# Gate logits of the last layer for seven of eight token groups, moved beside the second image's scan

## The chip, the cores and the metric

The kernel runs on one core of one Trainium2 chip, as one launch. The metric is device time in microseconds (us), and a kernel's time is the median of its runs. Everything is in float32.

## The reference, cut to what matters

The model takes two images of 128 channels on 64 x 64 points (4096 tokens each) through two layers. Layer 0 has a deformable convolution and a small mixture of experts. Layer 1 has a selective scan over the 4096 tokens and then the expert block that this change touches:

```
# layer 1: the scan, then the experts
x = x + _L1_conv_ref(_ln_c(x), ...)            # scan over tokens; its sum is x3 in the kernel
t = _to_tokens(x)
t = t + _L1_ffn_ref(_ln_t(t), gate_w, gate_b, weight1, weight2)

# _L1_ffn_ref, with 64 experts and K = 8
logits = einsum('bsd,ed->bse', x, gate_w) + gate_b
probs = softmax(logits, axis=1)                # over all 4096 tokens
vals, idx = top_k(probs.transpose(0, 2, 1), K) # eight tokens for each expert
pooled = einsum('bked,bke->bed', gathered, topv)
h = gelu(einsum('ebd,edh->ebh', [pooled, 1], weight1))
out = einsum('ebh,eho->ebo', [h, 1], weight2)
outputs[topi] += out * topv
```

The softmax runs over tokens, so it needs the logits of all tokens, and their maximum. The norm, the transposes and the logits of a token need that token alone.

## The kernel before

**The stages.** The deformable convolution of both images comes first. Then `L1Conv.scan` (L1549) runs over 16 pieces `k` of 512 tokens: pieces 0 to 7 are image 0, pieces 8 to 15 image 1. While image 0 is scanned, the rest of image 1's layer 0 and its first steps of layer 1 run beside it (the list `rest`). While image 1 is scanned, only work for its own next piece runs beside it. Last comes `L1Ffn.run`: the gate, the experts and the output.

**The scan loop.** Each piece has 32 units (two halves of 128 channels, 16 states each). A unit `u` issues, in this order: the scan itself on DVE (L1668); `drive(u + 3)`, a product on POOL (L1580); the copy of a state on POOL (L1677); `decay(u + 2)`, an exponential on ACT (L1587) into one of two PSUM tiles `da`; four transposes on PE of the unit before (`turn`, L120, two PSUM tiles `ht`); and `weigh(u - 2)`, a product with C, which for image 1 is one quarter on DVE (L1614) and three quarters on ACT (L1616). PE then adds the weighted tiles up by further transposes into `py` (L1625). Each engine takes its instructions in the order in which they were issued.

**The side work of the scan.** After these, a unit takes steps from a list `side` of generators: two steps a unit, and four in piece 7 once `rest` is done. Each generator stands for one piece of work and gives way at every `yield`:

- `prepare(k + 1)` (L1467) makes the next piece ready. It has 11 empty steps (L1485), then loads `zz` and `sab` and takes 37 more steps: eight convolution matmuls on PE (L1444), sigmoids on ACT (L1451 to L1459), products on POOL (L1462), the projection `px` on PE (L1500) and its copy on ACT (L1503), further small matmuls, then a softplus made of squares on ACT (L1537) and products on DVE (L1530 to L1544), and two products on POOL (L1547).
- `project(k - 1)` (L1701) is put ahead of it at unit 5 of each piece. It has five steps: a load of `xr`, 16 matmuls on PE (L1710), two empty steps, and an add on DVE (L1720) with the store of the 512 tokens to the tensor `x3` in device memory (L1721).

At unit 28 the list is drained, whatever is left in it. `prepare` has 48 steps and `project` five, so at two steps a unit they end in unit 26.

The transfers are issued on SP's queue, in order: among them are the rows `bcb` (L1598), one for each unit and eight units deep, each of which waits for a free buffer, so that SP is some five units ahead of the scan.

**Weights ahead.** The 64 experts' weights come in 16 chunks of four experts, 1 MB each, for `weight1` and again for `weight2`. A pool of `EARLY` = 9 buffers is opened during image 1's scan, and `ahead` (called every 24 units, L1664) loads a chunk into it. A pool of `LATE` = 4 buffers is loaded in the gate stage. So 13 chunks are in place or on their way when the experts begin, and the other 19 are loaded as buffers come free.

**The gate** (L1820). It loads all of `x3` in 16 transfers, then for each of eight groups of 512 tokens and each image takes the norm of the tokens (`token_norm`, L94 to L107, with a square root on ACT, L81), four transposes (L120), a copy (L1857) and a matmul with the gate weights (L1858); then the bias on ACT (L1861) and the group's maximum on DVE (L1847). Next come the maximum over the groups (L1867), one exponential over all logits (L1870), the eight largest (L1871, L1873), and the pooling of tokens (L1878 to L1897). This last part of the program, `L1Ffn.run`, is not in the order that is written by hand: there the framework orders the instructions.

Three helpers matter:

```
def rstd_gen(nc, out, var, eps):
    nc.vector.tensor_scalar(out, var, eps, None, ALU.add)
    nc.scalar.activation(out, out, AF.Sqrt)
    yield
    yield
    nc.vector.reciprocal(out, out)
```

`token_norm_gen` issues four pairs of `bn_stats` and `bn_aggr`, then the lines above, then four `tensor_scalar` and one `yield`; `token_norm` runs it through at once.

Of the kernel before, what the change touches and what calls it, by code (L numbers as in the profile page):

```python
# [19 lines left out]
P = 128  # L20
B = 2
# [4 lines left out]
GT = 4  # L26
# [86 lines left out]
def token_norm(*args):  # L113
    for _ in token_norm_gen(*args):
        pass
# [999 lines left out]
class L1Conv:  # L1115
# [351 lines left out]
    def prepare(self, b, k, sp, pp, res):  # L1467

        env, nc = self.env, self.env.nc
        l0 = k * LC  # L1470
        bank = lambda shape, name: pp.tile(shape, F32, name=name, tag="m")
        wk = lambda name: sp.tile([P, 2, LC], F32, name=name, tag="wk", bufs=3)
        xc = sp.tile([P, 2, LC + 3], F32, name="xc", bufs=1)
        xsd = self.xsd[b].rearrange("(h p) l -> p h l", p=P)
        if k:
            nc.sync.dma_start(out=xc, in_=xsd[:, :, l0 - 3 : l0 + LC])
        else:
            nc.gpsimd.memset(xc[:, :, 0:3], 0.0)
            nc.sync.dma_start(out=xc[:, :, 3:], in_=xsd[:, :, 0:LC])

        def gap(n):
            for _ in range(n):
                yield

        yield from gap(11)  # L1485
        zz = sp.tile([P, 2, LC], F32, name="zc")
        nc.sync.dma_start(out=zz, in_=self.zsd[b].rearrange("(h p) l -> p h l", p=P)[:, :, l0 : l0 + LC])
        sa = sp.tile([P, LC], F32, name="sab", tag="one", bufs=1)
        nc.sync.dma_start(out=sa, in_=self.sad[b][0, l0 : l0 + LC].partition_broadcast(P))

# [36 lines left out]
        nc.scalar.activation(e, v, AF.Abs)  # L1527
        nc.scalar.activation(e, e, AF.Exp, scale=-1.0)
        yield from gap(3)
        nc.vector.tensor_scalar(q, e, LINEAR[0], LINEAR[1], ALU.mult, ALU.add)  # L1530
        yield
        nc.vector.tensor_tensor(q, q, e, ALU.mult)
        dl = sp.tile([P, 2, LC], F32, name="delta")
        du = sp.tile([P, 2, LC], F32, name="du")
        ts = [dl, du] * 2
        for i, (sc, _, add) in enumerate(SQUARES):
            nc.scalar.activation(ts[i], e, AF.Square, bias=self.sqb[:, i : i + 1], scale=sc)  # L1537
            yield
# [12 lines left out]
    def scan(self, sp, ps, pp, rest, ahead):  # L1551
# [87 lines left out]
        def project(k):  # L1639
            return self.project(k // NK, k % NK, pieces[k]["zz"], sp, pp)  # L1640
# [11 lines left out]
        for u, (k, half, n) in enumerate(units):  # L1652
            state = states[k // NK]
            if k and half == 0 and n == 5:
                side.todo.appendleft(project(k - 1))
            last = n == DS - 4 and half == 1
            if last and k == NK - 1:
                rest.drain()
# [3 lines left out]
                side.add(gen)  # L1662
            fetch(u + BCB - 2)
            if k >= NK and u % 24 == 12:  # L1664
                ahead()

            hs[u] = sp.tile([P, LC], F32, name="h", bufs=3)
            nc.vector.tensor_tensor_scan(  # L1668
# [17 lines left out]
            if n == DS - 1:  # L1686
                adds.append((u + 4, gate, u))

            for _ in range(2 if rest.todo or k != NK - 1 else 4):
                side.step()  # L1690
            credit += 1
            while credit > 0 and rest.todo:
# [51 lines left out]
EC = 4  # L1744
EQ = 16
NHC = HID // P
EARLY = 9
LATE = 4


class L1Ffn:
# [1 line left out]

    def __init__(self, env, ctx):
        self.env, self.ctx = env, ctx
        self.early, self.w1 = None, []

    def fetch(self, pool):  # L1760
# [7 lines left out]
    def ahead(self):  # L1768

        if self.early is None:  # L1770
            self.early = self.ctx.enter_context(self.env.tc.tile_pool(name="f1x", bufs=EARLY, side="right"))
        if len(self.w1) < EARLY:
            self.fetch(self.early)

    def run(self, x3, out):
        tc, nc, d = self.env.tc, self.env.nc, self.env.d
        env = self.env
        with ExitStack() as ctx:
# [23 lines left out]
            with (  # L1802
# [3 lines left out]
                for i, (b, g) in enumerate(work):  # L1806
# [10 lines left out]
                    nc.vector.tensor_copy(so, flat)  # L1817
                    nc.sync.dma_start(out=out[b, :, g * 512 : (g + 1) * 512], in_=so)

    def gate(self, x3, G, s1, pd, late):  # L1820


        env, tc, nc, d = self.env, self.env.tc, self.env.nc, self.env.d
        with (
            tc.tile_pool(name="f1r", bufs=1) as rp,
            tc.tile_pool(name="f1s", bufs=2) as sp,
            tc.tile_pool(name="f1p", bufs=2, space=PSUM) as pp,
        ):
            xn = rp.tile([P, NT, B, C], F32, name="xn")
            for g in range(NG):  # L1830
                for b in range(B):
                    cut = slice(g * GT, (g + 1) * GT)
                    nc.sync.dma_start(out=xn[:, cut, b, :], in_=x3[b][:, cut, :])
            for _ in range(LATE):
                self.fetch(late)
            gw = rp.tile([P, B, B, E1], F32, name="gw")
            nc.gpsimd.memset(gw, 0.0)
            for b in range(B):
                nc.scalar.dma_start(out=gw[:, b, b, :], in_=d["gate_w"])
            gb = rp.tile([P, 1], F32, name="gb")  # L1840
            for b in range(B):
                nc.scalar.dma_start(out=gb[b * E1 : (b + 1) * E1, :], in_=d["gate_b"])
            lg = rp.tile([P, N], F32, name="lg")
            mx = rp.tile([P, NG], F32, name="mx")

            def largest(g):
                nc.vector.tensor_reduce(mx[:, g : g + 1], lg[:, g * 512 : (g + 1) * 512], AX.X, ALU.max)  # L1847

            for g in range(NG):
                pl = pp.tile([P, 512], F32, name="pl")  # L1850
                for b in range(B):
                    dst = xn[:, g * GT : (g + 1) * GT, b, :]
                    token_norm(env, sp, "n3", dst, dst, 1e-5)
                    pb = pp.tile([P, GT, P], F32, name="pb")
                    transpose4(nc, env.ident, pb, [dst[:, j, :] for j in range(GT)])
                    xnt = sp.tile([P, 512], F32, name="xnt")
                    nc.scalar.copy(xnt, pb.rearrange("p j t -> p (j t)"))  # L1857
                    nc.tensor.matmul(  # L1858
                        pl, gw[:, b, :, :].rearrange("p k e -> p (k e)"), xnt, start=b == 0, stop=b == B - 1
                    )  # L1860
                nc.scalar.activation(lg[:, g * 512 : (g + 1) * 512], pl, AF.Identity, bias=gb)  # L1861
                if g:
                    largest(g - 1)
            largest(NG - 1)
            m8 = rp.tile([P, 8], F32, name="m8")

            nc.vector.tensor_reduce(s1, mx, AX.X, ALU.max)  # L1867
# [117 lines left out]
def metaformer_kernel(ctx: ExitStack, tc: tile.TileContext, d: dict, out: bass.AP):  # L1985
# [2 lines left out]
    tile_d = lambda shape, name: [dp.tile(shape, F32, name=f"{name}{b}", tag=f"{name}{b}") for b in range(B)]  # L1988
    x2, x3 = tile_d([P, NT, C], "x2_"), tile_d([P, NT, C], "x3_")
    keep = ctx.enter_context(tc.tile_pool(name="keep", bufs=1))  # L1990
    last = L1Ffn(env, ctx)
    with tc.manual_schedule(engines={ET.PE, ET.DVE, ET.Activation, ET.Pool, ET.SP}), ExitStack() as l0:
        mixer = L1Conv(env, dp, keep, x2, x3)
        mixer.room = lambda: ctx.enter_context(tc.tile_pool(name="wd", bufs=1, side="right"))
# [14 lines left out]

        conv = L0Conv(env, l0)  # L2010
        conv.run(chain(mixer.constants(), position_matrices(env, mixer.pos)), after)
        mixer.run(functools.partial(after, 1), last.ahead)
    last.run(x3, out)


# [83 lines left out]
```

## Time and profile before

| | us |
|---|---|
| median of three runs (7286.02 to 7301.13) | 7298.4 |
| the profiled execution's own time | 7266.68 |
| its span, from the first to the last instruction | 7264.9 |
| image 1's first piece (k = 8), from 6449.9 | 74.6 |
| pieces 9 to 14, each | 72.3 to 75.1 |
| piece 15, from 6965.5 | 46.8 |
| gate: norms, logits and maxima, 7025.8 to 7072.1 | 46.3 |
| gate: softmax, eight largest, pooling, 7072.1 to 7112.3 | 40.2 |
| experts, from the first matmul at 7117.0 to 7237.2 | 120.2 |
| output, to the end | 27.7 |

A piece is counted from its first scan to the next piece's first scan. Times in the profile count from the first instruction. In a line of the timeline the first number is the start, the second the duration, then come the engine, the line, the operation and what it writes and reads; in square brackets stand the idle time of the engine before it and what ended it. In a line of a stretch (from:to) stand, for each engine, its busy time with the number of instructions, then the granted TensorE clock, the share of DMA time and GB/s.

### The profile page before, as it was taken

How to read it: one execution, taken by the hardware profiler on the slowest of the kernel's cores; microseconds unless marked ns; L12 is line 12 of the kernel's file. 1: busy time of each engine (PE TensorE's matmuls, PEld its weight loads, DVE VectorE, ACT ScalarE, POOL GpSimd, SP SyncE). 2: the span in 40 equal slices, each digit the busy share in tenths (PEclk: the TensorE clock that was granted, in tenths of full speed). 3: DMA queues.
4: the chain of work that ended last, by engine and by line, in shares of the span. 5: the costliest groups of instructions: out<-in, count | busy, mean ns of one | idle time of the engine just before them, and what ended most of it. 6: DMA issues, size and time to landing. Idle time of an engine off the chain costs nothing.

```text
span 7264.9 us, 72120 instructions
## 1 busy us (share of the span) xinstructions
PE 5060.9 (70%) x22497; PEld 3188.1 (44%) x22497; DVE 5800.1 (80%) x6710; ACT 2259.9 (31%) x4642; POOL 5081.6 (70%) x5062
## 2 busy tenths in 40 slices
PE   4667677777777665766666776766547888867768
PEld 3444444444444442333333443443224567755544
DVE  5988888888888887898988888788866766677871
ACT  2211111111111112311111222121118877677860
POOL 4777777777777777777777777777765345567840
PEclk8888898898888988988889888888878888888889
DMA  7887777777777778877777888878765234544545
GB/s 221 276 286 227 231 224 231 218 238 224 232 229 222 232 218 275 293 239 230 232 229 220 254 249 242 243 244 250 230 187 180 79 106 130 147 144 156 169 137 162
DMA packets 667321, 1550.06 MB, mean 213 GB/s; under 512 B 181668, under 2 KB 230988, under 8 KB 666940
## 3 DMA queue, kind: packets, MB, share of 16 engines
q0 software_dynamic: 307200, 1006.88, 46.0%
q1 hardware_dynamic: 330812, 490.87, 21.2%
q10 hardware_dynamic: 28928, 47.70, 1.8%
q8 instruction: 182, 2.98, 0.2%
q14 instruction: 199, 1.63, 0.1%
HBM read 1436.70 MB, written 110.84 MB: 213 GB/s over the span
## 4 chain that ended last, share of the span: by engine, by line
PE 45%; issue 20%; DVE 10%; DMA 10%; POOL 7%; ACT 6%; SPq 2%; ACTq 0%; DVEq 0%; POOLq 0%
PE out L799 20%; PE pst L120 6%; POOL v L731 6%; DMA v<-table,idx 6%; PE po L428 5%; DVE v L772 2%; DVE h L1668 2%; ACT w L1616 2%; PE ps L1234 1%; PE ht L120 1%; DVE v L774 1%; PE ps L1247 1%; PE px L1028 1%; PE py L1625 1%; PE pfo L875 1%
## 5 line engine op out<-in xcount | busy, mean ns | idle before, releaser
L731 POOL DMA_INDIRECT v<-table,idx x3840 | 4085.1, 1064 | 1264.4 <-issue 990.0
L772 DVE TENSOR_TENSOR v<-v,pw 128x2048 f32<-128x2048 f32 x960 | 2192.3, 2284 | 620.8 <-DMA v<-table,idx 561.7
L799 PE MATMUL out<-st,regw 128*128 128x512 f32 x3840 | 2213.5, 708 | 89.7 <-ACT ys L813 84.6
L779 ACT COPY st<-pst 128x512 f32<-128x512 f32 x960 | 561.7, 585 | 3967.3 <-PE pst L120 3947.6
L120 PE MATMUL pst<-ident,v 128*128 128x128 f32 x3840 | 690.0, 309 | 1556.9 <-issue 1374.1
L120 PEld LDWEIGHTS pst<-ident,v 128*128 128x128 f32 x3840 | 473.3, 156 | 1989.1 <-issue 1755.7
L774 DVE TENSOR_TENSOR v<-v 128x1024 f32<-128x1024 f32 x960 | 1176.9, 1226 | 33.1
L799 PEld LDWEIGHTS out<-st,regw 128*128 128x128 f32 x3840 | 787.4, 228 | 696.8 <-issue 587.1
L1580 POOL TENSOR_TENSOR db<-du,bcb 128x512 f32<-128x512 f32 x512 | 670.1, 1309 | 510.1 <-DVE h L1668 382.7
L1668 DVE TENSOR_TENSOR_SCAN h<-da,state,db 128x512 f32<-128x512 f32 x512 | 652.0, 1273 | 85.2 <-ACT da L1587 53.8
L775 DVE TENSOR_TENSOR v<-v 128x512 f32<-128x512 f32 x960 | 664.2, 692 | 33.0
L120 PE MATMUL ht<-ident,h 128*128 128x128 f32 x2048 | 364.6, 307 | 235.6 <-ACT w L1616 211.3
L1587 ACT ACTIVATE da<-delta,w_A_log 128x512 f32<-128x512 f32 x512 | 359.9, 703 | 220.0 <-DVE h L1668 216.3
L120 PEld LDWEIGHTS ht<-ident,h 128*128 128x128 f32 x2048 | 262.7, 157 | 364.4 <-ACT w L1616 301.0
L1616 ACT ACTIVATE w<-ht,ct 128x128 f32<-128x128 f32 x1280 | 384.1, 371 | 21.9 <-DVE w L1614 21.5
L428 PEld LDWEIGHTS po<-wa,win 128*128 128x128 f32 x2112 | 323.2, 200 | 96.2 <-issue 96.2
L1614 DVE TENSOR_TENSOR w<-ht,ct 128x256 f32<-128x256 f32 (+1 forms) x512 | 173.7, 339 | 230.6 <-PE ht L120 228.3
L428 PE MATMUL po<-wa,win 128*128 128x147 f32 x2112 | 345.2, 296 | 0.0
L1625 PE MATMUL py<-ident,w 128*128 128x128 f32 x2048 | 338.3, 296 | 0.0
L1625 PEld LDWEIGHTS py<-ident,w 128*128 128x128 f32 x2048 | 274.1, 156 | 23.0 <-issue 22.7
L1234 PEld LDWEIGHTS ps<-ipw,hs 128*120 128x120 f32 x1408 | 180.7, 196 | 86.3 <-ACT X L1181 55.4
L1234 PE MATMUL ps<-ipw,hs 128*120 128x128 f32 x1408 | 188.8, 287 | 40.8 <-ACT X L1181 35.8
(327 smaller groups left out, 5189.2 us busy)
## 6 DMA issues: line engine op xcount, KB each, us to landing
bcb<-bc SPq DMA_DIRECT2D x512, 256.0 KB
regw<-in_regw SPq DMA_DIRECT2D x192, 640.0 KB
v<-table,idx POOLq DMA_INDIRECT x3840
yd<-ys ACTq DMA_DIRECT2D x128, 256.0 KB
yc<-yd SPq DMA_DIRECT2D x16, 2048.0 KB
wt<-in_weight SPq DMA_DIRECT2D x32, 1024.0 KB
tm<-pos SPq DMA_DIRECT2D x32, 720.0 KB
pos<-zero SPq DMA_DIRECT2D x48, 240.0 KB
```

Of the source, the lines that this page charges most:

```text
L120: nc.tensor.transpose(ps[:, j, :], s, ident)
L428: m()
L731: self.env.nc.gpsimd.indirect_dma_start(out=v[:, j, :], out_offset=None, in_=self.table[b], in_offset=bass.IndirectOffsetOnAxis(ap=idx[:, ...
L772: nc.vector.tensor_tensor(v4, v4, w, ALU.mult)
L774: nc.vector.tensor_tensor(up, up, v4[:, :, 2:4, :], ALU.add)
L775: nc.vector.tensor_tensor(v4[:, :, 0, :], v4[:, :, 0, :], v4[:, :, 1, :], ALU.add)
L779: nc.scalar.copy(st, pt.rearrange("p j t -> p (j t)"))
L799: nc.tensor.matmul(self.out[half], self.regw[t // CH][:, t % CH, half * P : (half + 1) * P], st, start=first, stop=last,)
L1580: nc.gpsimd.tensor_tensor(dbs[u], pieces[k]["du"][:, half, :], rows.pop(u), ALU.mult)
L1616: nc.scalar.activation(ws[u][:, j, :], ht[:, j, :], AF.Copy, scale=ct[:, j, n : n + 1])
L1625: nc.tensor.matmul(py[k][:, j * P : (j + 1) * P], w[:, j, :], env.ident, is_transpose=True, start=False, stop=n == DS - 1 and j == GT - 1,)
L1668: nc.vector.tensor_tensor_scan(hs[u], das.pop(u), dbs.pop(u), state[:, half, n : n + 1], ALU.mult, ALU.add)
```

## The change

The norms, transposes, logits and maxima of the first seven groups are taken out of the gate and made a generator `logits(g)`, which joins the side list of the scan. It is added at unit 5 of pieces 9 to 15, for the group of the piece before (`g = k - 9`), behind whatever is in the list. It has 16 steps: the loads of both images' `x3` slices and four steps' wait; for each image the statistics and the root, an empty step, the reciprocal and the scalings, the transposes, and the copy; then both matmuls in one step, the bias in one, the maximum in one. The gate itself keeps group 7.

In pieces 9 to 15 a unit takes three side steps for two. For the pieces prepared there, `prepare` has 18 empty steps at its start for 11.

The pools of the gate (normed tokens `xn`, gate weights, logits, maxima) are opened in image 1's first piece, and their gate weights are loaded there on SP's queue (before: ACT's, in the gate). To make room, `EARLY` is 5 for 9, and `LATE` is 6 for 4: 11 chunks ahead for 13.

```diff
-        yield from gap(11)
+        yield from gap(18 if b and k > 1 else 11)
...
                 side.todo.appendleft(project(k - 1))
+                if k > NK:
+                    side.add(ahead.logits(k - 1 - NK, pp, "m"))
...
-                ahead()
+                ahead.ahead()
...
-            for _ in range(2 if rest.todo or k != NK - 1 else 4):
+            for _ in range((3 if k > NK else 2) if rest.todo or k != NK - 1 else 4):
                 side.step()
...
-EARLY = 9
-LATE = 4
+EARLY = 5
+LATE = 6
...
+    def logits(self, g, pp, tag=None):
+        env, nc, sp = self.env, self.env.nc, self.gp
+        bank = lambda shape, name: pp.tile(shape, F32, name=name, tag=tag or name)
+        cut = slice(g * GT, (g + 1) * GT)
+        for b in range(B):
+            nc.sync.dma_start(out=self.xn[:, cut, b, :], in_=self.x3[b][:, cut, :])
+        for _ in range(4):
+            yield
+        xnt = []
+        for b in range(B):
+            dst = self.xn[:, cut, b, :]
+            yield from token_norm_gen(env, sp, "n3", dst, dst, 1e-5)
+            pb = bank([P, GT, P], "pb")
+            transpose4(nc, env.ident, pb, [dst[:, j, :] for j in range(GT)])
+            yield
+            xnt.append(sp.tile([P, 512], F32, name="xnt"))
+            nc.scalar.copy(xnt[b], pb.rearrange("p j t -> p (j t)"))
+        yield
+        pl = bank([P, 512], "pl")
+        for b in range(B):
+            nc.tensor.matmul(pl, self.gw[:, b, :, :].rearrange("p k e -> p (k e)"), xnt[b], start=b == 0, stop=b == B - 1)
+        yield
+        at = self.lg[:, g * 512 : (g + 1) * 512]
+        nc.scalar.activation(at, pl, AF.Identity, bias=self.gb)
+        yield
+        nc.vector.tensor_reduce(self.mx[:, g : g + 1], at, AX.X, ALU.max)
+        yield
...
     def gate(self, x3, G, s1, pd, late):
...
-            tc.tile_pool(name="f1r", bufs=1) as rp,
-            tc.tile_pool(name="f1s", bufs=2) as sp,
+            self.gates,
...
             for _ in range(LATE):
                 self.fetch(late)
...
-            for g in range(NG):
-                pl = pp.tile([P, 512], F32, name="pl")
...
-            largest(NG - 1)
+            for _ in self.logits(NG - 1, pp):
+                pass
```

More of the change, by code (lines that the diff above doesn't have):

```diff
@@ L1746, with __init__ @@
 NHC = HID // P
-EARLY = 9
-LATE = 4
+EARLY = 5
+LATE = 6
 class L1Ffn:
-    def __init__(self, env, ctx):
-        self.env, self.ctx = env, ctx
+    def __init__(self, env, ctx, x3):
+        self.env, self.ctx, self.x3 = env, ctx, x3
         self.early, self.w1 = None, []
@@ L1771, in ahead @@
             self.early = self.ctx.enter_context(self.env.tc.tile_pool(name="f1x", bufs=EARLY, side="right"))
+            self.open_gate()
         if len(self.w1) < EARLY:
@@ L1818, in run, with open_gate @@
                     nc.sync.dma_start(out=out[b, :, g * 512 : (g + 1) * 512], in_=so)
+    def open_gate(self):
+        nc, d = self.env.nc, self.env.d
+        self.gates = ExitStack()
+        rp = self.rp = self.gates.enter_context(self.env.tc.tile_pool(name="f1r", bufs=1, side="right"))
+        self.gp = self.gates.enter_context(self.env.tc.tile_pool(name="f1s", bufs=2, side="right"))
+        self.xn = rp.tile([P, NT, B, C], F32, name="xn")
+        self.gw = rp.tile([P, B, B, E1], F32, name="gw")
+        nc.gpsimd.memset(self.gw, 0.0)
+        for b in range(B):
+            nc.sync.dma_start(out=self.gw[:, b, b, :], in_=d["gate_w"])
+        self.gb = rp.tile([P, 1], F32, name="gb")
+        for b in range(B):
+            nc.sync.dma_start(out=self.gb[b * E1 : (b + 1) * E1, :], in_=d["gate_b"])
+        self.lg = rp.tile([P, N], F32, name="lg")
+        self.mx = rp.tile([P, NG], F32, name="mx")
+    def logits(self, g, pp, tag=None):
[7 more added lines that the diff above has]
+        xnt = []
+        for b in range(B):
+            dst = self.xn[:, cut, b, :]
[7 more added lines that the diff above has]
+        pl = bank([P, 512], "pl")
+        for b in range(B):
+            nc.tensor.matmul(pl, self.gw[:, b, :, :].rearrange("p k e -> p (k e)"), xnt[b], start=b == 0, stop=b == B - 1)
[5 more added lines that the diff above has]
+        yield
     def gate(self, x3, G, s1, pd, late):
@@ L1824, in gate @@
         with (
-            tc.tile_pool(name="f1r", bufs=1) as rp,
-            tc.tile_pool(name="f1s", bufs=2) as sp,
+            self.gates,
             tc.tile_pool(name="f1p", bufs=2, space=PSUM) as pp,
         ):
-            xn = rp.tile([P, NT, B, C], F32, name="xn")
-            for g in range(NG):
-                for b in range(B):
-                    cut = slice(g * GT, (g + 1) * GT)
-                    nc.sync.dma_start(out=xn[:, cut, b, :], in_=x3[b][:, cut, :])
+            rp, sp, xn, lg, mx = self.rp, self.gp, self.xn, self.lg, self.mx
             for _ in range(LATE):
                 self.fetch(late)
[L1836 to L1849, printed above, removed]
-                pl = pp.tile([P, 512], F32, name="pl")
[L1851 to L1863, printed above, removed]
-            largest(NG - 1)
+            for _ in self.logits(NG - 1, pp):
+                pass
             m8 = rp.tile([P, 8], F32, name="m8")
@@ L1990, in metaformer_kernel @@
     keep = ctx.enter_context(tc.tile_pool(name="keep", bufs=1))
-    last = L1Ffn(env, ctx)
+    last = L1Ffn(env, ctx, x3)
     with tc.manual_schedule(engines={ET.PE, ET.DVE, ET.Activation, ET.Pool, ET.SP}), ExitStack() as l0:
@@ L2011, in metaformer_kernel @@
         conv.run(chain(mixer.constants(), position_matrices(env, mixer.pos)), after)
-        mixer.run(functools.partial(after, 1), last.ahead)
+        mixer.run(functools.partial(after, 1), last)
     last.run(x3, out)
```

## The prediction

> **What bounds the kernel now.** I read the stages first: busy time of each engine in single pieces of image 1's scan, then in the gate's first part. The columns are PE, PEld, DVE, ACT, POOL, the granted clock, DMA share and GB/s.
>
> ```profile
> 6673.30:6746.80 73.50, 52.29 (x304) 38.08 (x303) 57.44 (x75) 59.56 (x146) 58.66 (x73) 0.86 0.50 151
> 6965.50:7012.30 46.80, 37.49 (x277) 30.08 (x278) 45.72 (x68) 44.29 (x128) 40.74 (x63) 1.00 0.49 150
> 7025.80:7072.10 46.30, 31.15 (x96) 14.10 (x96) 41.51 (x232) 18.80 (x41) 0.00 (x0) 0.92 0.55 168
> ```
>
> A piece with preparation (the first line, piece 11) has some 15 us without work on each of DVE, ACT and POOL. Piece 15 (second line) prepares nothing, and there DVE is busy 45.7 of 46.8 us. The gate's part (third line) is bound by DVE: 41.5 of 46.3 us for eight groups. Whether the 15 us are free for other work is seen in the timeline, first in a smooth stretch, DVE and then ACT:
>
> ```profile
> 6674.70 1.27 DVE L1668 TENSOR_TENSOR_SCAN h<-da,state,db 128x512 f32<-128x512 f32 x1
> 6675.89 0.26 DVE L1614 TENSOR_TENSOR w<-ht,ct 128x128 f32<-128x128 f32 x1
> 6676.07 1.27 DVE L1668 TENSOR_TENSOR_SCAN h<-da,state,db 128x512 f32<-128x512 f32 x1
> ```
> ```profile
> 6674.64 0.70 ACT L1587 ACTIVATE da<-delta,w_A_log 128x512 f32<-128x512 f32 x1
> 6675.26 0.88 ACT L1616 ACTIVATE w<-ht,ct 128x128 f32<-128x128 f32 x3
> 6676.01 0.71 ACT L1587 ACTIVATE da<-delta,w_A_log 128x512 f32<-128x512 f32 x1
> ```
>
> A unit takes 1.37 us, DVE has no gap in it, and ACT's exponential and three products start after each other every 1.37 us too. Neither engine has room here. The 15 us are in the middle of the piece, in waits of the preparation:
>
> ```profile
> 6685.87 0.29 DVE L1614 TENSOR_TENSOR w<-ht,ct 128x128 f32<-128x128 f32 x1 [1.07 <-PE ht L120]
> ...
> 6707.10 1.28 DVE L1668 TENSOR_TENSOR_SCAN h<-da,state,db 128x512 f32<-128x512 f32 x1 [4.19 <-ACT da L1587]
> ...
> 6713.64 0.29 DVE L1614 TENSOR_TENSOR w<-ht,ct 128x128 f32<-128x128 f32 x1 [3.16 <-PE ht L120]
> ```
>
> The first is `project`'s matmuls ahead of the transposes, the second the sigmoids ahead of the exponential, the third `px`.
>
> **Where the new work falls.** At three steps a unit, `prepare` (18 + 37 = 55 steps) and `project` (5) fill 20 units, so the 16 steps of `logits` run in units 20 to 25: behind the preparation, in the smooth stretch that had no room. Nothing is left for the drain at unit 28.
>
> **What one group costs there.** From the gate's stretch a group has 41.51 / 8 = 5.2 us of DVE, 31.15 / 8 = 3.9 us of PE, and (18.80 - 1.28) / 8 = 2.2 us of ACT. The 1.28 is one table load; in the gate all roots run under it. In the scan each root stands between exponentials, and the trace shows what such a change of function costs:
>
> ```profile
> 6703.93 1.06 ACT L1459 ACTIVATE sg<-zc 128x1024 f32<-128x1024 f32 x1
> 6705.01 1.28 ACT L1587 ACT_TABLE_LOAD   x1
> 6706.31 0.69 ACT L1587 ACTIVATE da<-delta,w_A_log 128x512 f32<-128x512 f32 x1
> ```
>
> The two roots of a group are in units 21 and 22, with exponentials between, so there are four loads: 4 x 1.28 = 5.1 us, and ACT has 7.3 us for a group. The Trainium skill (ScalarE: Activation LUTs, What ACT_TABLE_LOAD costs) gives a load 1.28 us and a drain of 1.38 behind it, and speaks against scattered roots. By it the four switches would be 10.6 us and the sum below some 5.5 us a group higher. The rows show 0.02 us on either side of the load and no drain.
>
> I follow the queues of one group by the durations of these rows, in us from the end of unit 21's scan. ACT: exponential and products to 1.37, load to 2.65, root to 2.85, load to 4.13, exponential to 4.83. DVE: statistics 1.2 to 1.35, the next scan to 2.62, reciprocal and four scalings (1.25, after the root) to 4.1, the second image's statistics to 5.3, scan to 6.65, then it waits for the second root. ACT: products to 5.5, copy to 6.05, load 7.33, root 7.5, load 8.8, exponential 9.5. DVE: scalings to 8.8, two scans to 11.5. ACT's copy of the second image ends at 12.05, PE's two last passes of the logits (1.13) at 13.65, the bias (0.69) at 14.35. The maximum (0.69) stands on DVE ahead of the next scan and ends at 15.05. Undisturbed that scan starts at 0.1 + 4 x 1.37 = 5.6, so the group costs 9.5 us. With 0.5 for the handovers that I left out: 10 us. Below it cannot be less than DVE's 5.2, if all of ACT is hidden; above, 12.5 if DVE and ACT never overlap (5.2 + 7.3).
>
> Six such groups (pieces 9 to 14): 60 us, between 31 and 75. In piece 15 `logits` starts in unit 6, right behind the store of the tokens that it loads. The store's landing (2.0) and the load's (some 4 us in the gate, from 7021.56 to the first statistics at 7025.82) let DVE wait some 2 us, and matmuls, bias and maximum fall in one unit. Followed the same way it costs 13 us, between 8 and 16. SP waits for the store there too, some 2 us, with the rows `bcb` behind it; the scan is then late anyway.
>
> **What three steps a unit do to the preparation.** `project`'s add comes a unit earlier, ahead of the transposes that wait for its matmuls: of 1.07 us of waiting I keep 0.35, seven times, -5 us. For the rest two stretches of before stand beside each other. Piece 7 takes four steps a unit: units 9 to 14, which hold the chain from the sigmoids to the last product, take 6395.81 to 6423.69, 27.9 us, 18.8 above six units of 1.51. Piece 14 takes two: its units 13 to 24 take 6915.86 to 6955.50, 39.6 us, 23.2 above twelve of 1.37. Four steps were 4.4 us cheaper, since more of the chain's waits fall into the sigmoids' stall. I take half for three: -2.2 x 6 = -13 us. Ends: -26 (all of it), and +13, because image 0's ACT has a product less in each unit and hides more. `zz` and `sab` are loaded one unit earlier and used one unit earlier, as they were; seven empty steps cost no engine anything.
>
> **What the gate saves.** Before, the statistics start at 7025.82 and the last maximum ends at 7072.10:
>
> ```profile
> 7071.41 0.69 DVE L1847 TENSOR_REDUCE mx<-lg 128x1 f32<-128x512 f32 x1 [3.00 <-ACT lg L1861]
> 7072.13 0.16 DVE L1867 TENSOR_REDUCE s<-mx 128x1 f32<-128x8 f32 x1
> ```
>
> With one group left, image 1's slice lands as early as the first slice did, at 7025.8, and then goes through statistics (1.2), root and reciprocal (0.7), scalings (1.1), transposes (0.9), copy (0.6), matmul (1.15), bias (0.75) and maximum (0.7): 7.1, at 7033. Saved: 39 us, between 35 and 40. Softmax, pooling and experts follow earlier by as much; nothing in them is shorter.
>
> **Weights.** Two chunks fewer are ahead. PE takes a chunk every 3.43 us (eight passes of 0.43), and loads are issued as fast, each when a buffer is free (7130.14, 7133.58, 7137.01 in the trace). With eleven buffers a load has some eleven chunks' time for two rings of five and six; the tightest, the third to fifth chunk of `weight2`, wait for the chunks before them in a ring of five and still have 14 us. The six late ones are issued at 7022 for 7078 and move at some 300 GB/s, 21 us. I take 0; the price if a ring falls behind is 2 x 3.43 = 7 us up to some 25. Four loads fewer during the scan and seven pairs of 256 KB more: 0.
>
> **The sum.** 60 + 13 - 5 - 13 - 39 = +16 us. On the profiled execution's 7266.68 that is 7283; that execution ran 32 us under the median of the runs, 7298.4, and I put the +16 on the median: 7314. It is only just over what a measurement of this kernel tells from no change, 0.2% or 14.6 us.
>
> **The rivals.**
>
> *A: the new work hides itself; faster.* ACT's loads lie fully under DVE's statistics and scalings, so a group costs 5.2, and the faster preparation gives back all of 4.4. Then 31 + 8 - 5 - 26 - 39 = -33 us: 7265. For it: in image 0's scan units with statistics and a root have 0.2 us of DVE idle time. Against it: there ACT has only two products in a unit. It decides for faster once a group with its piece's gain costs less than (39 + 5 - 13) / 6 = 5 us net; I reckon 7.8. Chance 0.20.
>
> *B: DVE and ACT stand one behind the other, slower.* Each hands its delay to the other, since `da` and `ht` are two deep: 12.5 a group, no gain of pace. 75 + 16 - 39 = +52: 7350. For it: the equal 1.37 us of both queues. Chance 0.20.
>
> *C: weights late.* As the forecast, and the experts wait 7 to 25 us: 7321 to 7339. For it: loads as slow as PE takes them. Against: idle DMA from 7183 to 7213 before. Chance 0.10.
>
> *D: the gate's part does not shrink as it should,* because something else is late behind one group (the six weight loads ahead of it on SP, or the pools' room): 10 to 20 us less saved, 7324 to 7334. Chance 0.05.
>
> *Forecast:* 0.45; its own range +2 to +32, 7300 to 7330.
>
> **The numbers.** Range: from 7276 (most of A's way) to 7350 (B). Faster by over 0.2%: most of A, 0.18. Within 0.2%: two fifths of the forecast (0.18) and the rest of A (0.02), 0.20. Slower: the rest of the forecast (0.27), B, C and D, 0.62.
>
> **What would show it.** Pieces 9 to 14 should take 80 to 83 us for 73.6, with DVE idle ahead of L1847 (waiting for the bias) and L84 (for the root), and four more table loads in each; piece 15 some 59 for 46.8; the gate to its last maximum 7 to 8 us from the first statistics for 46.3; matmuls L1945 and L1965 without gaps. Wrong would be: pieces near 78 (A), near 86 (B), or experts over 122 us (C).

## The result, and the profile after

| | before | after |
|---|---|---|
| median, us (six runs each, side by side) | 7285.47 | 7354.21 |
| ratio, with its 95% interval | | 1.0092 [1.008, 1.0105] |
| pieces 9 to 14 together | 441.0 | 512.0 |
| piece 15 | 46.8 | 63.6 |
| from the last scan to the end | 252.6 | 229.5 |
| experts, from the first matmul to the output's first | 120.2 | 120.0 |

The kernel became 69 us slower, where 16 were forecast: the direction was right, and the time lies 4 us above the range. The spans of the two profiled executions, 7264.9 and 7357.6 us, differ by 92.7 us, of which 28 lie ahead of piece 8, where both run the same program; so I compare stretches. The changed part grew by 71.0 + 16.8 - 23.1 = 64.7 us. These are the stretches of after that answer to those of the prediction: piece 11, piece 15, and the gate from image 1's statistics to the last maximum (columns as there; image 0's half of group 7 was already normed in piece 15).

```profile
6723.20:6808.60 85.40, 59.55 (x316) 41.88 (x316) 63.38 (x105) 67.33 (x156) 57.01 (x74) 0.82 0.44 139
7064.60:7128.10 63.50, 46.67 (x289) 37.22 (x290) 56.18 (x111) 55.12 (x140) 40.62 (x61) 0.84 0.38 115
7157.60:7165.50 7.90, 3.32 (x6) 1.23 (x6) 3.37 (x16) 1.48 (x3) 0.00 (x0) 0.50 0.00 0
```

A piece takes 85.4 us for 73.5, though DVE has only 5.9 us more to do: the new work did not fill the 15 us in which it waits. The gate's last line is as short as forecast, 7.9 us, but it begins late. The timeline of SP's queue and then of DVE at the end of after's scan shows why:

```profile
7135.06 0.32 SPq L1723 DMA_DIRECT2D x<-xr  x1
7137.29 7.83 SPq L1767 DMA_DIRECT2D wt<-in_weight  x6
7145.17 2.48 SPq L1844 DMA_DIRECT2D xn<-x  x1
```
```profile
7157.66 0.49 DVE L94 BATCH_NORM_STATS2 n_st<-xn 128x6 f32<-128x128 f32 x2 [22.63 <-DMA xn<-x]
...
7159.57 1.12 DVE L107 TENSOR_SCALAR xn<-xn,n_mv,n_rs 128x128 f32<-128x128 f32 x4
7164.72 0.69 DVE L1864 TENSOR_REDUCE mx<-lg 128x1 f32<-128x512 f32 x1 [4.04 <-ACT lg L1862]
```

The last store of `x3` leaves SP at 7135.06. Then SP issues six weight chunks, and only behind them the slice that the last group needs; the data arrive 22.6 us after the store. Before, the first statistics followed the store by 7025.82 - 7019.26 = 6.6 us.

DVE's timeline in units 21 to 25 of piece 11 holds one group:

```profile
6783.06 0.28 DVE L94 BATCH_NORM_STATS2 n_st<-xn 128x6 f32<-128x128 f32 x1
...
6784.77 0.24 DVE L80 TENSOR_SCALAR n_rs<-n_mv 128x4 f32<-128x4 f32 x1
6784.93 1.27 DVE L1670 TENSOR_TENSOR_SCAN h<-da,state,db 128x512 f32<-128x512 f32 x1
...
6786.50 1.90 DVE L107 TENSOR_SCALAR xn<-xn,n_mv,n_rs 128x128 f32<-128x128 f32 x4
6788.32 0.28 DVE L94 BATCH_NORM_STATS2 n_st<-xn 128x6 f32<-128x128 f32 x1
...
6799.74 0.69 DVE L1864 TENSOR_REDUCE mx<-lg 128x1 f32<-128x512 f32 x1 [3.41 <-ACT lg L1862]
```

The statistics of one image fill 1.87 us (6783.06 to 6784.93), four scalings 1.90; the maximum waits 3.41 us for the biased logits, and the scans stand behind it. DVE waits for neither root: in pieces 9 to 14 the profile shows no idle time ahead of the reciprocals, though each of these pieces has six table loads for two before, as forecast.

### The profile page after: what moved, and what is told of

Read it like the earlier page. It is cut to its first block, busy times and chain, and to the rows that moved or that the text cites. A ratio compares the mean times of both kernels' runs of the same rounds, so it can differ in the third digit from the quotient of the medians.

```text
span 7357.6 us, 72099 instructions
## 1 busy us (share of the span) xinstructions
PE 5103.8 (69%) x22497; PEld 3223.1 (44%) x22497; DVE 5807.2 (79%) x6710; ACT 2302.3 (31%) x4672; POOL 5081.5 (69%) x5062
```

## The experiments

My theories were: (1) the order on SP's queue, not the group's own chain, made the gate late; (2) the faster pace of side steps saves nothing; (3) a group's price is DVE's own work and the one wait, not ScalarE's table loads. The rivals stand in each expectation. The runs were made on several chips, on which the kernel before took from 7275 to 7622 us; each ratio is to the kernel before on the same chip. Stretches are compared across chips: the pieces of the changed kernel's scan take 85.3 us on three of them, while the kernel before was profiled on one alone.

**1. The slices first (e1_slice_first).**

```diff
+            last = self.logits(NG - 1, pp)
+            next(last)
             for _ in range(LATE):
                 self.fetch(late)
-            for _ in self.logits(NG - 1, pp):
+            for _ in last:
                 pass
```

> Changed kernel with one edit: group 7's two slice loads are issued ahead of the six late weight loads instead of behind them. Theory (SP's order): in the changed kernel the image-1 slice lands 22.5 us after x3's last store because SP issues six weight loads between them (7.83 + 2.54 + 2.75 us); with the slices first the last group maximum comes some 16 us earlier, the rest after piece 15 falls from 229.4 to about 213 us, and the time to 7338 us. Rival (the time goes to the group's own chain of statistics, root, transposes, logits, or the slices wait for the same DMA engines anyway): under 4 us, 7350 to 7354. Second rival: the weights, now later, hold the experts: their stretch grows from 120 to over 125 us and the gain is given back.

Measured: 1.0063 [1.0041, 1.0084]. Pieces 85.3, piece 15 63.6, the rest 213.0 us for after's 229.5: 16.5 us less, as theory (1) has it. SP's queue and DVE of this run:

```profile
7411.25 0.32 SPq L1723 DMA_DIRECT2D x<-xr  x1
7413.25 0.37 SPq L1844 DMA_DIRECT2D xn<-x  x1
7413.93 10.01 SPq L1767 DMA_DIRECT2D wt<-in_weight  x6
```
```profile
7416.52 0.49 DVE L94 BATCH_NORM_STATS2 n_st<-xn 128x6 f32<-128x128 f32 x2 [5.30 <-DMA xn<-x]
...
7423.58 0.69 DVE L1864 TENSOR_REDUCE mx<-lg 128x1 f32<-128x512 f32 x1 [4.04 <-ACT lg L1862]
```

The slice lands 5.3 us after the store. Against the kernel before, the part behind the scan is now 252.6 - 213.0 = 39.6 us shorter: the forecast's 39, once the order is right. The weights, issued later, delay nothing.

**2. The pace alone (e2_pace_alone)**, on the kernel before:

```diff
-        yield from gap(11)
+        yield from gap(18 if b and k > 1 else 11)
...
-            for _ in range(2 if rest.todo or k != NK - 1 else 4):
+            for _ in range((3 if k > NK else 2) if rest.todo or k != NK - 1 else 4):
```

> Kernel before with the pace alone: image 1's pieces put 18 units between the parts of the preparation and take three side steps a unit, no group of logits beside the scan, the weights as before. The prediction's terms for it: 5 us less from project's first addition and 2.2 us a piece over six pieces, together 18 us less, pieces 9 to 14 at about 70.5 us and a time of 7267 us. Rival (what the changed kernel's pieces suggest, 85.3 less 11.8 us of the group is 73.5 us, the mean of the kernel before): pieces 73 to 74.5 us, and a time within 5 us of 7285.

Measured: 1.002 [1.0008, 1.0031], 6 to 23 us slower. Pieces 9 to 14 take 450.7 us for 441.0, that is 75.1 each, and piece 15 1.1 more. Neither number of the forecast holds, and the rival's "no change" is still a little too good. DVE's waits in piece 11 (what waited, for whom, sum, times, longest), first before, then this run:

```profile
DVE w L1614 <- PE ht L120: 7.6, 7, 3.2
DVE h L1668 <- ACT da L1587: 4.2, 1, 4.2
DVE h L1668 <- POOL state L1677: 2.6, 2, 1.5
DVE q L1530 <- ACT e L1528: 0.9, 1, 0.9
DVE q L1540 <- ACT delta L1537: 0.4, 1, 0.4
```
```profile
DVE w L1614 <- PE ht L120: 8.7, 5, 2.0
DVE h L1668 <- ACT da L1587: 3.0, 1, 3.0
DVE q L1530 <- ACT e L1528: 2.6, 1, 2.6
DVE xr L1720 <- PE po L1710: 1.9, 1, 1.9
DVE h L1668 <- POOL state L1677: 1.8, 2, 1.1
DVE q L1540 <- ACT du L1537: 1.3, 1, 1.3
```

The faster pace puts fewer scan units between the links of one chain, and the chain waits instead: for `po` 1.9 us, for `e` 2.6 in place of 0.9, for the squares 1.3 in place of 0.4. It shortens the wait for `da` by 1.2. In image 0's piece 7, my model for it, the mix of work is another.

**3 and 4. The table loads (e3_no_root), and the wait for the bias (e4_spread).** In run 3 the root of groups 0 to 6 is a copy; in run 4 bias and maximum come later.

```diff
-    nc.scalar.activation(out, out, AF.Sqrt)
+    nc.scalar.activation(out, out, f)
...
-            yield from token_norm_gen(env, sp, "n3", dst, dst, 1e-5)
+            yield from token_norm_gen(env, sp, "n3", dst, dst, 1e-5, f=AF.Copy if tag else AF.Sqrt)
```

> Changed kernel in which the root of the norms of groups 0 to 6 (beside the scan) is a plain copy on ScalarE: the square root is left out there, so no activation table is loaded for it. Theory (VectorE's own work sets the price of a group, the table loads lie in ScalarE's idle time): pieces 9 to 14 within 1 us of 85.3 us, and a time of 7347 to 7356 us. Rival (the four table loads of 1.28 us a group push ScalarE's queue, and through the bias's wait of 3.41 us VectorE): 3 to 5 us less a piece, 80 to 82 us, and a time of 7318 to 7335 us.

```diff
-        yield
+        for _ in range(4):
+            yield
         nc.scalar.activation(at, pl, AF.Identity, bias=self.gb)
-        yield
+        for _ in range(4):
+            yield
         nc.vector.tensor_reduce(self.mx[:, g : g + 1], at, AX.X, ALU.max)
```

> Changed kernel in which the bias follows the logits' matrix product by four side steps instead of one, and the maximum follows the bias by four instead of one; nothing else is changed. Theory (the 3.41 us that VectorE waits in unit 25 for the biased logits is an effect of the order on VectorE's queue alone): the wait falls under 0.5 us, pieces 9 to 14 fall from 85.3 to about 82.3 us, the time to about 7333 us. Rival (ScalarE or VectorE is short of time in that stretch as a whole, and the wait only moves on to the next unit's products): pieces stay above 84.5 us, the time above 7347 us.

Measured: 1.0099 [1.0075, 1.0123] and 1.0078 [1.0056, 1.01]. Read by the pieces alone, both settle on 85.3 us again (only piece 14 of run 4 is shorter, 83.2): theory holds for the loads, the rival for the wait. Read by units, that is too simple (us, piece 11 but for the last row):

| | units 13-16 | units 20-27 | piece |
|---|---|---|---|
| pace alone (run 2) | 17.14 | 12.65 | 75.1 |
| after | 16.74 | 22.79 | 85.4 |
| no root | 18.15 | 21.79 | 85.3 |
| spread | 19.00 | 20.66 | 85.4 |
| both (run 5, piece 13) | 20.74 | 20.68 | 85.4 |

Units 20 to 27 give the price of a group, 22.79 - 12.65 = 10.1 us. Against run 2, DVE is busy 7.9 us more in piece 11 (63.38 for 55.51) and waits 3.4 for the bias, while its other waits are 1.4 shorter together:

```profile
6965.70:7040.80 75.10, 53.65 (x304) 38.53 (x304) 55.51 (x76) 59.70 (x147) 56.94 (x74) 0.84 0.49 153
```

Without the loads units 20 to 27 are 1.0 shorter, and that is the same wait (2.41 us for 3.41 in piece 11); without the wait they are 2.1 shorter, and without both no more than that. Yet the piece stays as long: units 13 to 16, where nothing was edited, grow by about as much. They range from 16.7 to 18.6 us between the pieces of after alone, but the means over pieces 9 to 14 are 17.5 us in after, 18.7 in run 3 and 19.4 in run 4. So something else seems to hold the length. TensorE's granted clock changes only on a grid of 3.413 us, and 85.33 us are 25.00 steps of it; run 2's 75.09 us are 22.00. The pieces of before are 21.2 to 22.0 steps long and differ.

**5. Both at once (e10_root_and_spread)**, on the kernel of run 1:

> The kernel of run e1_slice_first with both edits of runs e3 and e4 at once: the roots of groups 0 to 6 are plain copies (the square root is left out there), and bias and maximum follow four side steps later. Each edit alone took 1 and 2 us out of units 20 to 27, which came back in units 13 to 16, at 25.00 of the clock's windows of 3.413 us a piece. Theory (the clock's grid holds the piece until enough is taken away): with some 3 us out of units 20 to 27 the piece leaves 85.3 us and falls to 22 to 24.5 windows, 75 to 83.5 us; time 10 to 60 us under that of e1. Rival (something else of 85.3 us length bounds the piece): 85.3 us again.

Measured: 1.0046 [1.003, 1.0061]; against run 1 some 2 us less in pieces 9 to 14 together, 4 in piece 15 and 2 behind it. Pieces 9 to 14: 83.8, 84.1, 85.8, 85.4, 85.4, 85.4. My theory that taking enough away frees the piece was not borne out: it began at 24.5 steps and then settled at 25.0, and the two edits together took only 2.1 us out of units 20 to 27, where I had reckoned with 3. What gives the time back can be seen in unit 16, first in piece 11 of after, then here in piece 13: the same products on TensorE, DVE's wait behind them, and the clock of the grid steps around them (the value behind the five busy times).

```profile
6759.34 2.11 PE L1519 MATMUL pd<-xd,dtw 8*128 8x512 f32 x4
...
6762.54 0.29 DVE L1614 TENSOR_TENSOR w<-ht,ct 128x128 f32<-128x128 f32 x1 [2.04 <-PE ht L120]
```
```profile
6757.66:6761.07 3.41, 3.41 (x19) 1.97 (x17) 2.73 (x4) 1.56 (x5) 3.41 (x5) 1.00 0.68 184
6761.07:6764.48 3.41, 3.41 (x16) 3.10 (x16) 0.29 (x1) 3.29 (x8) 2.52 (x4) 0.50 0.96 312
```
```profile
7248.56 3.78 PE L1519 MATMUL pd<-xd,dtw 8*128 8x512 f32 x4
...
7253.42 0.29 DVE L1614 TENSOR_TENSOR w<-ht,ct 128x128 f32<-128x128 f32 x1 [4.13 <-PE ht L120]
```
```profile
7246.85:7250.26 3.41, 3.41 (x10) 2.20 (x10) 1.48 (x2) 0.12 (x1) 3.41 (x6) 0.50 0.94 275
7250.26:7253.68 3.42, 3.42 (x10) 1.75 (x9) 0.26 (x1) 2.92 (x7) 1.20 (x2) 0.50 0.93 285
```

At half clock the products take 3.78 us for 2.11, and DVE waits 4.13 us for 2.04. My reading is that a piece that gets shorter shifts against the grid, so that its half-clock steps fall on other work, and it pays there. What these lines show is the place and the price in one unit; that the grid holds the piece's length, and by which rule a step gets its clock, is not shown.

**6. TensorE kept busy with dummy products.** Two kernels have dummies in all slow units, one on the kernel of run 1 (e5_warm_after) and one on the kernel before (e6_warm_before); a third has a lighter set on the kernel before (e8_warm_light). Each also has two or three dummies ahead of `px`; these and the table `WARM` are left out here.

```diff
             hts[u] = ps.tile([P, GT, P], F32, name="ht")
+            k = units[u][0]
+            if NK <= k < 2 * NK - 1:
+                for _ in range(WARM.get(u % 32, 0)):
+                    flat = hts[u].rearrange("p j t -> p (j t)")
+                    nc.tensor.matmul(flat, env.ident, env.zero, start=True, stop=True)
```

> The kernel of run e1_slice_first plus dummy matrix products of zeros (128x512, two passes) on TensorE in image 1's slow units: one to three ahead of the transposes of units 13 to 25, into the tile that these overwrite, and three ahead of px. Nothing reads them. The granted clock changes on a grid of 3.413 us, and in this case's traces a window with less than about 1.5 us of matmuls at full clock is followed by one at half clock; the pieces of the changed kernel last 25.0 windows, the same with the roots out or the bias spread. Theory (the clock holds the length: the group thins TensorE's work in the window from 65 us on, the next two run at half clock): with the dummies the clock stays at 0.95 or more, pieces 9 to 14 leave 85.3 us and fall to 79 to 83 us, time 15 to 40 us under that kernel. Rival (VectorE's and ScalarE's own work sets 85.3 us and the clock only follows): the clock rises, pieces stay within 1 us of 85.3 us. Second rival: the dummies stand in the way of real products on TensorE's queue, pieces above 87 us.

> The kernel before with the same dummy products in image 1's slow units. Theory (clock): the windows at half clock (20 to 27 us of each piece) go, pieces 9 to 14 fall from 73.5 to 69 to 72 us, time 10 to 25 us under the kernel before. Rival (TensorE's speed is hidden behind VectorE's and ScalarE's waits there): pieces 73 to 74 us, no change of time. Second rival: the dummies delay real products, pieces above 75 us, slower.

> The kernel before with fewer dummy products: two in units 17 and 18, one in units 19 to 22, two ahead of px. Theory (clock): at about 8 of these 10 a piece the long stretch at half clock (some 14 of the 20 to 27 us) goes and most of the gain of run e6 stays, pieces 70.5 to 73 us. If the heavier dummies stood in the way there, this one is the faster of the two. Rival (hidden): pieces 73 to 74 us, no change.

Measured: 1.0097 [1.0071, 1.0123], 1.0112 [1.0086, 1.0138] and 1.0033 [1.002, 1.0045]. The clock rises to 0.96 to 1.00, 0.94 and 0.89, and yet the pieces grow, to 86 to 89, 85 to 86 and 77 to 79 us. The second rival holds: the dummies stand in the way (in the first, four of the six pieces are above its 87 us). Piece 11 of the second kernel (stretch, and DVE's first wait), where `ht` alone costs 19.8 us for 7.6:

```profile
6718.60:6804.00 85.40, 71.55 (x354) 44.93 (x354) 57.96 (x75) 60.50 (x147) 59.39 (x73) 0.94 0.44 133
```
```profile
DVE w L1626 <- PE ht L120: 19.8, 11, 5.7
```

So they don't say what a full clock alone would bring. In two pieces of the first, 10 and 12, the clock is 1.00 throughout. There the four products of the logits take 1.88 us for 3.37 at a mean clock of 0.56 in after, and the bias's wait is 2.59 us for 3.41. So 0.8 us of this wait goes with the clock, in a kernel in which the dummies move other things too.

**7. Two dummies only (e12_warm_two):**

> The kernel of run e1_slice_first with only two dummy products of zeros a piece, one in unit 23 and one in unit 24, where TensorE was busy 1.50 of 3.41 us in the window from 65.2 us on and the next two windows ran at half clock. Theory (the half clock there lengthens the logits' products, so the bias and VectorE's 3.41 us of waiting): the windows from 68.6 to 75.4 us stay at full clock, the wait in unit 25 falls by 1 to 2 us, pieces 9 to 14 fall below 85 us unless the clock's grid gives it back in units 13 to 16. Rival (the clock there is only a follower): wait and piece as before within 0.5 us.

Measured: 1.0068 [1.0048, 1.0087]. The half-clock steps did not vanish; they moved to 28.8 to 62.9 and 73.2 to 76.6 us, and the wait stayed at 3.39 us in piece 11. The pieces alternate, 87.6 and 86.5, together 174.1 us or 51.0 steps. In every other one (10, 12 and 14) the logits' products ran at a clock of 1.00: they took 1.88 us, and the wait was 2.58 to 2.61 us. That is the same 0.8 us as in run 6, less than the 1 to 2 us of the theory, and these pieces were 1.2 us longer than run 1's all the same. So the clock has a share in the wait, and a shorter wait did not make a shorter piece.

**8. The groups at the old pace (e7_old_pace)**, both pace lines of run 2 undone in the kernel of run 1:

> The kernel of run e1_slice_first with the pace of the kernel before: two side steps a unit and 11 empty steps, so that what is left of a group's steps at unit 28 is drained there at once. Theory (the three-step pace costs 1.6 us a piece, as run e2 showed by 75.1 against 73.5 us): pieces 9 to 14 about 83 to 84 us if they leave the 25 windows of the clock, and about 10 us less time. Rival: the drained steps stand one behind the other (loads done, but root, transposes, copy, products, bias and maximum in one unit) and a piece costs more, 86 to 89 us, 5 to 20 us slower than that kernel.

Measured: 1.0082 [1.0057, 1.0108]; pieces 88.5, 86.2, 87.6, 85.8, 85.4, 85.3, on average 1.1 us longer than in run 1, and the wait for the bias is 4.70 us in piece 11 for 3.44. Piece 15 and what follows are 4.2 us shorter, so the whole is 2.6 us longer. The rival's way is the right one, though only the first three pieces reach its 86 us: without the faster pace what is left of a group falls into the drain at unit 28. The same pace that costs 1.6 us a piece alone (run 2) is worth 1.1 where a group stands at the end of the list.

**9. Group 7's slices in a tile of the gate (e11_late_slices):**

```diff
+            tc.tile_pool(name="f1l", bufs=1) as xp,
         ):
+            self.xl = xp.tile([P, GT, B, C], F32, name="xl")
...
```

> The kernel of run e1_slice_first in which group 7's normed tokens have a tile of their own in a pool that is opened in the gate, so that image 0's half of group 7's norm can't be taken into piece 15. Theory (of the 16.8 us that piece 15 is longer, what lies above the 13 forecast is that half: four pairs of statistics, four scalings and two table loads): piece 15 falls from 63.6 to 58 to 61 us; the gate's part, which waits for image 1's slice anyway, is at most 1 us longer; 2 to 5 us less in all. Rival (the norm filled waits of piece 15 and cost nothing): piece 15 stays within 1 us of 63.6 us and the gate gets 1 to 3 us longer.

Measured: 1.0059 [1.0042, 1.0075]. Piece 15 61.9 us, 1.7 less; the part behind it 215.2 for 213.0, 2.2 more. Piece 15 lies in neither range, but on balance the rival holds: the half norm that the framework took into piece 15 cost there about what it saved later. Without it group 6 costs 61.9 - 46.8 = 15.1 us, of which 1.1 are the pace's.

**10. Nearly the same work in the waits (e9_in_stalls).** Pace and empty steps as before; groups 0 to 5 in pieces 9 to 14, but each part of a group in the unit where its engine waits, with one root for both images; groups 6 and 7 in the gate, their slices ahead of the weights. The edit, cut to where the parts are taken:

```diff
+PARTS = (8, 12, 13, 15, 16, 19, 20, 23, 24, 25, 26)
...
                 side.step()
+            if NK < k < 2 * NK - 1 and u % 32 in PARTS:
+                if u % 32 == PARTS[0]:
+                    part = ahead.part(k - 1 - NK, pp)
+                next(part, None)
```

> A version meant to beat both kernels: pace and empty steps of the kernel before; groups 0 to 5 beside the scan (pieces 9 to 14), groups 6 and 7 in the gate, their slice loads ahead of the six late weight loads; nothing of a group in piece 15. A group's steps stand where VectorE or ScalarE waits: loads in unit 8, image 0's statistics in unit 12, image 1's in unit 13 with one root for both images right behind the sigmoids, scalings in units 15 and 16, transposes in 19 and 20, copies in 23 and 24, products in 24 and 25, bias in 26, the maximum in the next piece's unit 15. Theory (a group's price is not its work but where it stands): pieces 9 to 14 at 75 to 77 us for 73.5 (bias 0.7, what of the scalings does not fit the waits 1, one more table load partly given back by the wait for px), piece 15 back at 46.8, the gate some 32 to 35 us shorter than before: 15 to 25 us under the kernel before. Rival (the work itself is the price: about 10 us a group wherever it stands, or the clock's grid takes back what the waits give): pieces above 80 us, and a time above that of the kernel before by 5 us or more.

Measured: 0.9963 [0.995, 0.9976], some 28 us under the kernel before (some 24 by the two medians and by the stretches). Pieces 9 to 14 take 74.9 to 75.5 us, piece 15 46.8, and the part behind the scan 218.2 us, 34.4 less than before. DVE in piece 11 (the stretch; parts of its timeline; its two largest waits):

```profile
6975.80:7050.70 74.90, 56.60 (x317) 40.08 (x316) 66.20 (x103) 62.59 (x152) 59.44 (x73) 0.84 0.48 159
```
```profile
7001.37 0.86 DVE L1857 BATCH_NORM_STATS2 qst<-xn 128x6 f32<-128x128 f32 x4
7002.15 0.36 DVE L1859 BATCH_NORM_AGGREGATE qmv<-qst 128x2 f32<-128x6 f32 x4
...
7009.04 0.20 DVE L1867 RECIPROCAL qrs<-qrs 128x8 f32<-128x8 f32 x1 [1.92 <-ACT qrs L1863]
7009.28 2.10 DVE L1872 TENSOR_SCALAR xn<-xn,qmv,qrs 128x128 f32<-128x128 f32 x4
```
```profile
DVE w L1617 <- PE ht L120: 4.9, 7, 1.2
DVE qrs L1867 <- ACT qrs L1863: 1.9, 1, 1.9
```

DVE is busy 66.2 us for before's 57.4, 8.8 more, and the piece is 1.4 longer: the waits for `ht` fell from 7.6 to 4.9 us, that for `da` from 4.2 to none, and the new work stands in them. Over the six pieces a group costs 1.7 us; at the end of the list it cost 10.1. Not all of the difference is the place: one root for two and a maximum that comes later are part of it, and in runs 3 to 5 they were worth some 2 us together. These pieces average 22.0 steps of the grid, so how much of the 1.7 us is the grid's is open.

## Why the prediction was wrong

| step | forecast | measured | by |
|---|---|---|---|
| six groups | +60 | +60.8 | 6 x 10.14, units 20 to 27 of run 2 and of after |
| pace | -5 and -13 | +9.7 | run 2 |
| piece 15 | +13 | +16.8 | after |
| gate | -39 | -23.1 | after; -39.6 in run 1 |
| weights | 0 | in the line above | experts 120.0 for 120.2 |
| sum | +16 | +64.2 | +64.7 in the trace |

**The pace** is the largest miss, 27.7 us. "Four steps were 4.4 us cheaper, since more of the chain's waits fall into the sigmoids' stall. I take half for three" carried image 0's piece 7 over to image 1; run 2 shows new waits of 1.9, 1.7 and 0.9 us in the chain instead. I had +13 as the other end of this term, and chose against it. "Of 1.07 us of waiting I keep 0.35" had the wrong sign: in place of the 1.07 the add waits 1.9 us for its own matmuls. The first two rows hold in this order only: at the old pace the groups cost 77.8 us, and beside them the faster pace gave back 6.8 (run 8).

**The gate**: "image 1's slice lands as early as the first slice did" failed. SP reached that slice behind six weight loads, 10 us of issuing and a transfer behind them. I had named this as rival D at 0.05 and priced it at 10 to 20 us; it cost 16.5. In the working I gave the six loads' issue time (7022) and never asked what stands behind them on SP.

**The group** came out right in sum, partly by luck, and its parts did not. Statistics were put at 1.2 us an image and take 1.87, for in the gate two images' are interleaved (0.26 from one pair to the next) and here each aggregate follows its own statistics (0.40). Scalings were 1.1 and take 1.9 beside a product on POOL. The waits for the roots that I had followed through both queues did not occur in these pieces. The maximum's wait for the bias, 3.41, makes up for it. And after's piece is three whole steps of the grid longer than run 2's, 10.24 us; runs 3 and 4 made a group 1.0 and 2.1 us cheaper in its own units, and the piece did not get shorter. A group that is 1 or 2 us cheaper thus shows the same price, and the agreement with my 10 says little for my working.

**Piece 15**: the group does land there as forecast, and the term was 13 for 16.8; 1.1 comes from the pace (run 2) and 1.7 from group 7's half norm, which the gate gave back (run 9). The last 1.0 stays open; the wait for the loaded slice, put at some 2 us, was 1.1.

**Left out altogether**: the clock. I read its column and had no term for it. TensorE's four passes of the logits ran at a mean clock of 0.56 and took 3.37 us, where I had 1.13 for the last two. What a group or the pace would cost off the grid no run shows, since run 2 and after are each in step with it (22 and 25 steps); and runs 3, 4 and 5 could not be read by their times.

Rivals A and C did not happen. A's thought, that work can be hidden, is what run 10 shows, at other places than the change chose. Pieces "near 86" were my mark for B, and the mark was met by half of B: "no gain of pace" came true, but a group cost 10.1 and not 12.5, and DVE did not wait for the roots. Two slips of my working changed nothing here: A's terms add up to -31 and not -33, and by them A's pieces would stay near 73.5, so "near 78" was no mark of A.

## What to carry to other kernels

Idle time of an engine is room only for instructions that stand in its queue just ahead of the wait: a group cost 10.1 us at the end of the list, and nearly the same work 1.7 us spread over the waits. Before you price a transfer, write down what its queue issues between the event that allows it and the transfer itself. And read an experiment by stretches as well as by its total, since a loop can settle at a whole number of the clock's steps, as six kernels did here, and give back elsewhere what an edit saves.

## What the runs showed of the hardware that was not expected

**Loops in step with the clock.** Six kernels settled at 25.00 steps of 3.413 us a piece, three of them with different edits in the group (run 4 in five of its six pieces, run 5 in the last three); run 2 settled at 22.00, run 7 at 51.0 for two pieces. Others did not settle on whole steps, the kernel before among them. The Trainium skill (TensorE: Matmul & The Clock Gate, What's actually happening) names a free-running window of 3413 ns and two clock states; the grid and the values 1.00 and 0.50 of these traces agree. It also says that one busy window brings the full clock back. In after a half-clock step with TensorE busy 3.42 us (from 6795.19 on) is followed by one at 1.00. In run 5 TensorE is busy for three steps on end at half clock (3.41, 3.41 and 3.42 us from 7243.44 on) and the step after them is at 0.50 still; there the measurement decides. Busy time in the profile may not be what the window counts; no run here tells the two apart.

**Two engines, one port.** Four scalings took 1.12 us in the gate (7159.57) and 1.90 us beside the scan. There the first of them starts at 6786.50, takes 1.13 us, where the others take 0.33, and ends 0.08 us after POOL's product:

```profile
6786.28 1.27 POOL L1580 TENSOR_TENSOR db<-du,bcb 128x512 f32<-128x512 f32 x1 [1.16 <-DVE h L1670]
```

The Trainium skill (SBUF — State Buffer, Who interferes with whom) says that such a scaling on VectorE can take the port pair that it shares with GpSimd, and that the one that comes second is blocked until the other is through. The 0.8 us more agree with it, POOL being 0.2 us ahead.
